# Narrower logit tiles, and softmax sums and weighted values issued behind the next window's logits

## The chip, the cores and the metric

The kernel runs on one core of a Trainium2 chip. The metric is the device time of one execution in microseconds. The engines go by their short names: PE is the matrix engine, PEld its weight loads, DVE the vector engine, ACT the scalar engine, POOL the general one, and SP the engine whose queue issues most of the DMAs.

## The reference

The input is `x`, four images of 128 channels and 64x64 pixels in float32. The first layer normalises over channels, adds a 3x3 depthwise convolution, and cuts each image into sixteen 16x16 windows. In every window, for two branches of four heads of 32 channels, each pixel attends to its 5x5 neighbours inside the window:

```python
q = einsum('ncij,bhdc->nbhdij', xw, Wq)          # k and v likewise
logits = einsum('nbhdij,nbhdkij->nbhkij', q, patches(k, 5)) * HD ** -0.5
attn = softmax(logits, axis=3)                   # over the 25 neighbours
o = einsum('nbhkij,nbhdkij->nbhdij', attn, patches(v, 5))
x = x + mix_of_branches(einsum('nbhdij,bhcd->nbcij', o, Wo))
```

Neighbours that fall outside the window have a key of zero, so they add one each to the softmax sum and nothing to its values.

The second layer takes the pixels of an image as 4096 tokens: linear attention with elu+1 features and a cumulative state, `t = t + attn(ln(t))`, and then a recurrent layer over all tokens, `t = t + rnn(ln(t))`, whose input is batch-normalised.

## The kernel before

An image is cut into four bands of 16 rows (`bands`, 16 in all) and a band into four windows (`places`, 64 in all; `wj` is the window's place in its band). One pass of the main loop, called an iteration here and named by the `wj` of the window `i` whose logits it computes, works on several windows at once: logits of window `i`, sums and weighted values of window `i-1` (`weighted`), the division by the sums for window `i-2` (`scaled`), and the projections q, k, v of window `i+1` (`window_inputs`).

- `logits` adds a mask product (L377, bfloat16) and six products of keys and queries for each head (L382, float32) in one PSUM bank per head. A head's 32 channels use 32 rows of PE, and the 128 keys of a block all its 128 columns. ACT takes the exponential of each bank (L391, `es`).
- `weighted` multiplies `es` by ones for the softmax sums (L400) and by the values (L412), both on all 128 rows with 32 columns a head. ACT copies the sums out (`den`, L403) and the values (`o_sb`, L420). A DMA folds `den` to 128x16 (`dc`, L405), DVE adds the count of outside neighbours and inverts (L423 to L427), a DMA writes the result to DRAM (`rd`, L429) and another spreads it back over 128 partitions (`rden`, L431). `weighted` is a generator of three parts: the sums, the values, and the way from `dc` to `rden`.
- `scaled` multiplies `o_sb` by `rden` on POOL (L440), one iteration later, into `oT`, a band's attention output.
- The layer-1 work of a finished band is a list of 24 steps in `layer1`: output product (`output0`, L465, which reads `oT` of all four windows, and the sum L472), norms (`measure`: L191, L193 on DVE, L195, L196 on POOL; `norm`: L203), transposes (L212), features (L494, L496, L498, L499), scores (L537, L539), values (L511, L519), states (L554, L562), `attend` (L573, L575, and on DVE L583, L584, L587), `keep` (L212, L592, a store) and `product` (L602, L603, L604). It begins in the iteration with `wj=1`.
- The norm and convolution of the next band (`front`) is another such list; its eight taps a half band on DVE are L288 (`y`), and ACT copies the finished half (`y2w`, L324).
- `between(i, gap)` takes the next step of both lists. There are six gaps in an iteration. L400 stands between gaps 0 and 1, L412 between gaps 1 and 2, and the three parts of `window_inputs` (q and k at L337, v at L350 with two DMAs of `v_sb` at L359 and L360) ahead of gaps 3, 4 and 5.

`in_order` pins the order in which PE, DVE, ACT and POOL instructions were written; SP's queue and the PSUM banks (one pool of eight, `bank`) are placed by the scheduler. `rden`, `den` and `oT` have one buffer each. After the main loop a recurrent part runs for about 100 us; it is not touched.

Of the kernel before, what the change touches and what calls it, by code (L numbers as in the profile page):

```python
# [17 lines left out]
P = 128  # L18
# [4 lines left out]
WT = WS * WS  # L23
BR, HEADS, HD = 2, 4, 32
KR = 2
BLOCKS = ((0, 6, 0), (6, 10, 4), (10, 16, 8))
BAND = WS * W
NCH = BAND // P
# [18 lines left out]
def conv_attn_hybrid(ctx: ExitStack, tc: tile.TileContext, ins: dict, out: bass.AP):  # L47
    nc = tc.nc
# [9 lines left out]
    def loaded(name, shape, dt=F32, src=None, eng=None):  # L58
        t = const.tile(shape, dt, name=name)
        (eng or nc.sync).dma_start(t, ins[name] if src is None else src)  # L60
        return t
# [34 lines left out]
    def load_head(n):  # L96
        b, wi = bands[n]
        heads[n] = p1.tile([P, P], F32, tag="head", name="head")
        nc.sync.dma_start(heads[n], ins["xt"][b, wi, :, 0, :])
# [18 lines left out]
    mask_k = loaded("mask_k", [P, P], BF16, eng=nc.scalar)  # L118
    mask_q = loaded("mask_q", [P, BR * WT], BF16, eng=nc.scalar)
# [56 lines left out]
    def bank():  # L176
        return ps.tile([P, 512], F32, tag="bank", name="bank")

    def run(g):
        for _ in g:  # L180
            pass
# [181 lines left out]

    pieces = [(br, n) for br in range(BR) for n in range(len(BLOCKS))]

    def spans(br, n):
        r0, r1, key0 = BLOCKS[n]
        return slice(br * WT + r0 * WS, br * WT + r1 * WS), br * WT + key0 * WS

    def logits(w):  # L370


        sps = [bank() for _ in range(HEADS)]
        for h in range(HEADS):
            rows = slice(h * HD, (h + 1) * HD)

            nc.tensor.matmul(sps[h], mask_k[rows], mask_q[rows], start=True, stop=False)  # L377
        for br, n in pieces:
            cols, k0 = spans(br, n)
            for h in range(HEADS):  # L380
                rows = slice(h * HD, (h + 1) * HD)
                nc.tensor.matmul(  # L382
                    sps[h][:, cols],
                    w["k"][rows, k0 : k0 + P],
                    w["q"][rows, cols],
                    start=False,
                    stop=(br, n) == pieces[-1],
                )
        for h in range(HEADS):
            es = p2.tile([P, BR * WT], F32, tag=f"es{h}", name=f"es{h}")  # L390
            nc.scalar.activation(es, sps[h], AF.Exp, scale=scale)  # L391
            w["es", h] = es

    def weighted(w):


        ops, dps = bank(), bank()
        for h in range(HEADS):
            rows = slice(h * HD, (h + 1) * HD)
            nc.tensor.matmul(dps[rows], ones[:, :HD], w["es", h], start=True, stop=True)  # L400

        den = p1.tile([P, BR * WT], F32, tag="den", name="den")
        nc.scalar.copy(den, dps)  # L403
        dc = p2.tile([P, 16], F32, tag="dc", name="dc")
        nc.sync.dma_start(dc, den[::HD, :])  # L405
        yield
        for br, n in pieces:
            cols, _ = spans(br, n)
            for h in range(HEADS):
                rows = slice(h * HD, (h + 1) * HD)  # L410
                c0 = br * P + h * HD
                nc.tensor.matmul(  # L412
                    ops[rows, cols],
                    w["v"][:, n, c0 : c0 + HD],
                    w["es", h][:, cols],
                    start=(br, n) == pieces[0],
                    stop=(br, n) == pieces[-1],
                )
        o_sb = p2.tile([P, BR * WT], F32, tag="o_sb", name="o_sb")
        nc.scalar.copy(o_sb, ops)  # L420
        yield

        nc.vector.tensor_tensor(dc, dc, pad_c, ALU.add)  # L423
        rc = p2.tile([P, 16], F32, tag="rc", name="rc")
        nc.vector.reciprocal(rc, dc)
        nc.vector.tensor_tensor(dmax, dmax, dc, ALU.max)
        nc.vector.tensor_tensor(dmin, dmin, dc, ALU.min)  # L427
        rd = dram4.tile([HEADS, BR * WT], F32, tag="rd", name="rd")
        nc.sync.dma_start(rd.rearrange("h (a e) -> (h a) e", e=16), rc)  # L429
        rden = p1.tile([P, BR * WT], F32, tag="rden", name="rden")  # L430
        nc.sync.dma_start(rden, rd.unsqueeze(1).to_broadcast([HEADS, HD, BR * WT]))  # L431
        w["o"], w["rden"] = o_sb, rden
        yield
# [174 lines left out]
    def layer1(n, last):  # L608

        a, c = Half(n, 0), Half(n, 1)  # L610
        y, z = last
        order = [
            (keep, z), None,
            (norm, z), (product, y), None,
            (output0, a), (measure, a), None,
            (turn_last, z), None,
            (norm, a), (output0, c), (measure, c), None,
            (turn, a), None,
            (product, z), (norm, c), None,
            (queries, a), None,  # L620
            (keys, a), None,
            (turn, c), None,
            (values, a), None,
            (queries, c), None,
            (scores, a), None,
            (keys, c), None,
            (turn_keys, a), None,
            (values, c), None,
            (accumulate, a), None,
            (turn_keys, c), None,  # L630
            (attend, a, 0), None,
            (attend, a, 1), (measure, a), None,
            (scores, c), (keep, a), None,
            (accumulate, c), (norm, a), None,
            (attend, c, 0), None,
            (turn_last, a), (attend, c, 1), (measure, c), None,
        ]
        for what in order:
            if what is None:
                yield  # L640
            elif what[1] is not None:
                what[0](*what[1:])
        halves[n] = a, c
# [15 lines left out]
    places = [(n, wj) for n in range(len(bands)) for wj in range(NB)]  # L659
# [27 lines left out]
    windows = {0: {}}  # L687
# [4 lines left out]
    def between(i, gap):  # L692


        next(behind, None)
        if i < len(places) and (i == 0 or i % NB or gap in (0, 2, 4)):
            next(ahead, None)

    for i in range(len(places) + 2):
        if i < len(places):  # L700
            n, wj = places[i]
            if i and wj == 0 and n + 1 < len(bands) and bands[n + 1][1] < NB - 1:
                load_head(n + 2)
            logits(windows[i])
        if 2 <= i:
            m, wjm = places[i - 2]
            if wjm == NB - 1:
                run(behind)
                behind = layer1(m, halves.pop(m - 1, (None, None)))
        between(i, 0)  # L710
        if 2 <= i:
            scaled(m, wjm, windows.pop(i - 2))
        if i < len(places) and wj == 1 and n + 2 < len(bands):
            load(n + 2)
        sums = weighted(windows[i - 1]) if 1 <= i <= len(places) else iter(())
        for gap in (1, 2):
            next(sums, None)
            between(i, gap)
        run(sums)
        if i == 0:  # L720
            run(fourth)
        inputs = iter(())
        if i + 1 < len(places):
            windows[i + 1] = {}
            inputs = window_inputs(windows[i + 1], *places[i + 1])
        for gap in (3, 4, 5):
            next(inputs, None)
            between(i, gap)
        run(inputs)
    run(behind)  # L730
    run(layer1_end(*halves.pop(len(bands) - 1)))
# [82 lines left out]
    for r, (s, counts) in enumerate(rounds):  # L814
# [4 lines left out]
        for g, (c0, c1) in enumerate(halves):  # L819
# [6 lines left out]
                start=False,  # L826
                stop=True,
# [621 lines left out]
def _neighbours():  # L1449
# [6 lines left out]
    for a in range(NQT):  # L1456
        for q in range(QT):
            r, c = a * QROWS + q // WS, q % WS
            n = 0
            for y in range(max(r - KR, 0), min(r + KR, WS - 1) + 1):  # L1460
                for x in range(max(c - KR, 0), min(c + KR, WS - 1) + 1):
                    band[:, q, a, (y - QKEY0[a]) * WS + x] = 0.0
                    n += 1
            pad_n[:, q, a] = (2 * KR + 1) ** 2 - n
    pad_n = pad_n.reshape(P, NQT)
# [3 lines left out]
def _masks():  # L1469
# [10 lines left out]
    pad = np.zeros((1, BR, WT), np.float32)  # L1480
    for r0, r1, key0 in BLOCKS:
        for q in range(r0 * WS, r1 * WS):
            r, c = divmod(q, WS)
            for i in range(8):
                queries[:, i, :, q] = 0.0 if abs(key0 + i - r) <= KR else -BIG
            for j in range(WS):
                queries[:, 8 + j, :, q] = 0.0 if abs(j - c) <= KR else -BIG
            rows = min(r + KR, WS - 1) - max(r - KR, 0) + 1
            cols = min(c + KR, WS - 1) - max(c - KR, 0) + 1
# [57 lines left out]
```

## Time and profile before

| | us |
|---|---|
| median of 3 runs | 929.56 (928.55 to 930.22) |
| profiled execution, first to last instruction | 933.3 |
| PE busy | 878.8 (94% of the span) |
| DVE busy | 734.2 (79%) |
| ACT busy | 539.5 (58%) |
| POOL busy | 257.5 (28%) |
| POOL idle until `rden` has landed, L440 | 221.5, in 29 waits |

No other time of the profiled execution is given, so its own time is taken to be the span, 933.3 us; that is 3.7 us above the median of the runs. The first row comes from runs, the others from one profiled execution. In lines of the profile "128x512 f32 x4" is the shape and the number of instructions; a mean or a duration follows, and brackets name idle time of the engine just ahead and who ended it. Float32 products are two instructions each on PE. A line of the table by stretches gives the stretch, its length, the busy time and number of instructions of PE, PEld, DVE, ACT and POOL, the granted PE clock as a share of full speed, and the DMA share with its GB/s.

### The profile page before, as it was taken

How to read it: one execution, taken by the hardware profiler on the slowest of the kernel's cores; microseconds unless marked ns; L12 is line 12 of the kernel's file. 1: busy time of each engine (PE TensorE's matmuls, PEld its weight loads, DVE VectorE, ACT ScalarE, POOL GpSimd, SP SyncE). 2: the span in 40 equal slices, each digit the busy share in tenths (PEclk: the TensorE clock that was granted, in tenths of full speed). 3: DMA queues.
4: the chain of work that ended last, by engine and by line, in shares of the span. 5: the costliest groups of instructions: out<-in, count | busy, mean ns of one | idle time of the engine just before them, and what ended most of it. 6: DMA issues, size and time to landing. Idle time of an engine off the chain costs nothing.

```text
span 933.3 us, 26460 instructions
## 1 busy us (share of the span) xinstructions
PE 878.8 (94%) x10508; PEld 657.1 (70%) x10508; DVE 734.2 (79%) x2408; ACT 539.5 (58%) x1010; POOL 257.5 (28%) x358
## 2 busy tenths in 40 slices
PE   4968999999999999999999999999999999977894
PEld 3846787777787777778777777777777778755452
DVE  6454888889797879798888889787878787577694
ACT  3654656575656565665657575656666565522553
POOL 2112141323222232314132323323231403131174
PEclk9988999999999999999999999999999999989898
DMA  4111112122212121211212121212121111111853
GB/s 121 25 46 57 42 51 58 56 59 63 59 48 61 48 66 49 73 38 57 55 54 60 59 60 48 62 51 65 48 71 37 60 36 56 36 35 32 351 223 143
DMA packets 53045, 63.46 MB, mean 68 GB/s; under 512 B 22960, under 2 KB 33840, under 8 KB 52400
## 3 DMA queue, kind: packets, MB, share of 16 engines
q1 hardware_dynamic: 51184, 56.91, 19.6%
q10 hardware_dynamic: 1728, 4.77, 1.3%
q8 instruction: 85, 1.39, 0.7%
q14 instruction: 48, 0.39, 0.1%
HBM read 35.44 MB, written 17.30 MB: 57 GB/s over the span
## 4 chain that ended last, share of the span: by engine, by line
PE 59%; DVE 25%; DMA 5%; ACT 3%; issue 3%; POOL 3%; ACTq 0%; SPq 0%; DVEq 0%; POOLq 0%
DVE y L288 9%; PE bank L337 9%; PE bank L465 7%; PE bank L382 6%; PE bank L212 6%; PE bank L494 5%; PE bank L400 4%; PE bank L350 4%; PE bank L412 3%; PE bank L602 3%; DMA res<-resd 2%; DVE st L191 2%; PE bank L537 2%; DVE state L562 2%; DVE x L587 2%
## 5 line engine op out<-in xcount | busy, mean ns | idle before, releaser
L288 DVE SCALAR_TENSOR_TENSOR y<-ypad,cpe_w,y 128x512 f32<-128x512 f32 x240 | 191.5, 798 | 17.4 <-ACT y L286 13.9
L391 ACT ACTIVATE es<-bank 128x512 f32<-128x512 f32 x256 | 132.2, 603 | 77.3 <-PE bank L382 77.3
L440 POOL TENSOR_TENSOR oT<-o_sb,rden 128x512 f32<-128x512 f32 x64 | 83.9, 1311 | 247.3 <-DMA rden<-rd 221.5
L195 POOL TENSOR_SCALAR rs<-mv 128x4 f32<-128x4 f32 (+2 forms) x100 | 25.0, 250 | 366.1 <-DVE mv L193 162.8
L203 DVE TENSOR_SCALAR xn<-x,mv,rs 128x128 f32<-128x128 f32 x256 | 89.5, 411 | 26.5 <-POOL rs L196 26.5
L196 POOL TENSOR_TENSOR rs<-rs,mhalf 128x4 f32<-128x4 f32 (+2 forms) x100 | 106.3, 1063 | 8.3
L382 PEld LDWEIGHTS bank<-q,k 32*128 32x128 f32 x3072 | 97.8, 189 | 9.7 <-ACT k L345 8.5
L382 PE MATMUL bank<-q,k 32*128 32x96 f32 (+1 forms) x3072 | 96.3, 271 | 1.1 <-ACT k L345 1.1
L412 PEld LDWEIGHTS bank<-es,v_sb 128*32 128x32 f32 x3072 | 56.5, 110 | 30.0 <-issue 19.6
L465 PE MATMUL bank<-woT,oT 128*128 128x128 f32 x512 | 67.1, 287 | 6.8 <-POOL oT L440 6.8
L465 PEld LDWEIGHTS bank<-woT,oT 128*128 128x128 f32 x512 | 63.8, 200 | 10.8 <-POOL oT L440 8.5
L494 PE MATMUL bank<-xl,awT 128*128 128x512 f32 x128 | 70.0, 630 | 0.0
L412 PE MATMUL bank<-es,v_sb 128*32 128x96 f32 (+1 forms) x3072 | 69.7, 239 | 0.0
L337 PE MATMUL bank<-y2w,wqT 128*128 128x256 f32 x256 | 68.2, 390 | 1.0 <-DVE y2w L288 1.0
L357 ACT COPY v_sb<-bank 128x512 f32<-128x512 f32 x64 | 37.5, 586 | 54.7 <-PE bank L350 48.0
L400 PE MATMUL bank<-es,ones 128*32 128x512 f32 x512 | 68.9, 611 | 0.0
L337 PE MATMUL bank<-y2w,wkT 128*128 128x256 f32 x256 | 66.9, 385 | 0.0
L350 PE MATMUL bank<-wvT,y2w 128*128 128x256 f32 x256 | 66.4, 382 | 0.0
L345 ACT COPY q<-bank 128x512 f32<-128x512 f32 x64 | 37.6, 587 | 43.3 <-PE bank L337 41.2
L345 ACT COPY k<-bank 128x512 f32<-128x512 f32 x64 | 37.3, 583 | 37.6 <-PE bank L337 37.6
L191 DVE BATCH_NORM_STATS2 st<-x 128x6 f32<-128x128 f32 x256 | 55.5, 280 | 1.1
L337 PEld LDWEIGHTS bank<-y2w,wqT 128*128 128x128 f32 x256 | 46.7, 198 | 13.0 <-issue 7.2
(118 smaller groups left out, 1719.7 us busy)
## 6 DMA issues: line engine op xcount, KB each, us to landing
rden<-rd SPq DMA_DIRECT2D x64, 256.0 KB
v_sb<-v_sb SPq DMA_DIRECT2D x128, 64.0 KB
resd<-rs_o SPq DMA_DIRECT2D x32, 256.0 KB
out<-ot SPq DMA_DIRECT2D x32, 256.0 KB
xin<-in_xt SPq DMA_DIRECT2D x15, 512.0 KB
res<-resd SPq DMA_DIRECT2D x2, 2048.0 KB
res<-resd ACTq DMA_DIRECT2D x2, 2048.0 KB
dc<-den SPq DMA_DIRECT2D x64, 8.0 KB
```

Source lines behind the costliest of these rows:

```text
L196: nc.gpsimd.tensor_tensor(rs[:, :n], rs[:, :n], mhalf[:, :n], ALU.pow)
L203: nc.vector.tensor_scalar(xn[:, j, :], piece, mv[:, j, 0:1], rs[:, j : j + 1], ALU.subtract, ALU.mult)
L288: nc.vector.scalar_tensor_tensor(y2, src, cpe_w[:, tap : tap + 1], y2, ALU.mult, ALU.add)
L337: nc.tensor.matmul(pps[:, br * WT : (br + 1) * WT], wT[:, br * P : (br + 1) * P], y2, start=True, stop=True,)
L350: nc.tensor.matmul(vps[:, e * 256 : (e + 1) * 256], y2[:, e * P : (e + 1) * P], wvT, start=True, stop=True,)
L382: nc.tensor.matmul(sps[h][:, cols], w["k"][rows, k0 : k0 + P], w["q"][rows, cols], start=False, stop=(br, n) == pieces[-1],)
L391: nc.scalar.activation(es, sps[h], AF.Exp, scale=scale)
L400: nc.tensor.matmul(dps[rows], ones[:, :HD], w["es", h], start=True, stop=True)
L412: nc.tensor.matmul(ops[rows, cols], w["v"][:, n, c0 : c0 + HD], w["es", h][:, cols], start=(br, n) == pieces[0], stop=(br, n) == pieces[-1],)
L440: nc.gpsimd.tensor_tensor(oTs[n][:, :, :, wj * WS : (wj + 1) * WS], w["o"].rearrange("p (a r c) -> p a r c", a=BR, c=WS), w["rden"].rearra ...
L465: nc.tensor.matmul(yps[:, j * P : (j + 1) * P], oT[:, br, t], woT[:, br, :], start=br == 0, stop=br == BR - 1,)
L494: nc.tensor.matmul(zps, awT[:, m * P : (m + 1) * P], h.xl, start=True, stop=True)
```

## The change

The masks and logits are issued as tiles of 32 rows by 64 columns, so that each of their products becomes two, one for each half of the keys, into the two halves of the bank's partitions. The first `yield` of `weighted` is taken out, so its first part now holds the sums and the values. That part is run directly behind `logits`, ahead of gap 0, and its last part (`dc` to `rden`) behind gap 3.

```diff
+KC = 64
...
         for h in range(HEADS):
             rows = slice(h * HD, (h + 1) * HD)
 
-            nc.tensor.matmul(sps[h], mask_k[rows], mask_q[rows], start=True, stop=False)
+            for c in range(0, P, KC):
+                nc.tensor.matmul(
+                    sps[h][c : c + KC],
+                    mask_k[rows, c : c + KC],
+                    mask_q[rows],
+                    start=True,
+                    stop=False,
+                )
         for br, n in pieces:
             cols, k0 = spans(br, n)
             for h in range(HEADS):
                 rows = slice(h * HD, (h + 1) * HD)
-                nc.tensor.matmul(
-                    sps[h][:, cols],
-                    w["k"][rows, k0 : k0 + P],
-                    w["q"][rows, cols],
-                    start=False,
-                    stop=(br, n) == pieces[-1],
-                )
+                for c in range(0, P, KC):
+                    nc.tensor.matmul(
+                        sps[h][c : c + KC, cols],
+                        w["k"][rows, k0 + c : k0 + c + KC],
+                        w["q"][rows, cols],
+                        start=False,
+                        stop=(br, n) == pieces[-1],
+                    )
...
         nc.sync.dma_start(dc, den[::HD, :])
-        yield
         for br, n in pieces:
...
             logits(windows[i])
+        sums = weighted(windows[i - 1]) if 1 <= i <= len(places) else iter(())
+        next(sums, None)
         if 2 <= i:
...
-        sums = weighted(windows[i - 1]) if 1 <= i <= len(places) else iter(())
         for gap in (1, 2):
-            next(sums, None)
             between(i, gap)
-        run(sums)
...
         for gap in (3, 4, 5):
             next(inputs, None)
             between(i, gap)
+            run(sums)
         run(inputs)
```

## The prediction

> **What bounds the kernel now.** I read the page's busy times first, then a table of one band cut at its four L377 starts, then the order of time of PE, DVE, POOL and SP in that band, and last the waits.
>
> ```profile
> PE 878.8 (94%) x10508; PEld 657.1 (70%) x10508; DVE 734.2 (79%) x2408; ACT 539.5 (58%) x1010; POOL 257.5 (28%) x358
> ...
> 312.46:326.42 13.96, 13.55 (x175) 11.06 (x174) 13.26 (x58) 7.36 (x14) 4.70 (x7) 1.00 0.18 55
> ...
> sum 50.07, PE 49.66 PEld 37.95 DVE 42.55 ACT 30.84 POOL 13.57; mean PE 12.42 PEld 9.49 DVE 10.64 ACT 7.71 POOL 3.39
> ```
>
> A band lasts 50.07 us and PE is busy in 49.66, so PE bounds it. But DVE needs 42.55, and in the iteration with wj=0 (the line 312.46) it is busy 13.26 of 13.96 us: there two engines are full at once. DVE's order of time shows where it waits in a band; two of these waits open its long runs:
>
> ```profile
> 293.96 0.69 DVE L604 BATCH_NORM_STATS2 stats<-wx 128x6 f32<-128x512 f32 x1 [1.79 <-ACT wx L603]
> ...
> 303.98 0.74 DVE L288 SCALAR_TENSOR_TENSOR y<-ypad,cpe_w,y 128x512 f32<-128x512 f32 x1
> ...
> 306.86 0.43 DVE L498 TENSOR_SCALAR low<-low 128x512 f32<-128x512 f32 x1 [1.54 <-ACT low L496]
> ...
> 319.44 0.61 DVE L587 SCALAR_TENSOR_TENSOR x<-bank,rd,x 128x128 f32<-128x128 f32 x2
> ```
>
> From L498 at 306.86 to the end of L587 at 320.05 it has no gap: 13.19 us of queue. PE's order of time shows who waits for that, SP's and POOL's the way from dc to the output product:
>
> ```profile
> 312.69 1.48 PE L382 MATMUL bank<-q,k 32*128 32x96 f32 x48
> 314.10 0.71 PE L573 MATMUL bank<-v,aT 128*128 128x129 f32 x4
> 314.96 1.07 PE L400 MATMUL bank<-es,ones 128*32 128x512 f32 x8
> 317.05 1.09 PE L412 MATMUL bank<-es,v_sb 128*32 128x96 f32 x48
> 318.07 1.16 PE L537 MATMUL bank<-f,f 128*128 128x128 f32 x8
> 319.85 0.59 PE L212 MATMUL bank<-ident,x 128*128 128x128 f32 x2 [0.41 <-DVE x L587]
> ```
> ```profile
> 322.40 0.14 DVE L423 TENSOR_TENSOR dc<-dc,pad_c 128x16 f32<-128x16 f32 x1
> 322.86 0.33 SPq L429 DMA_DIRECT2D rd<-rc  x1
> 324.35 0.57 SPq L431 DMA_DIRECT2D rden<-rd  x1
> 325.46 0.51 SPq L359 DMA_DIRECT2D v_sb<-v_sb  x1
> 330.46 1.28 POOL L440 TENSOR_TENSOR oT<-o_sb,rden 128x512 f32<-128x512 f32 x1
> 332.48 2.05 PE L465 MATMUL bank<-woT,oT 128*128 128x128 f32 x16
> ```
> ```profile
> POOL oT L440 <- DMA rden<-rd: 221.5, 29, 13.6
> ```
>
> The reader is to see that oT ends at 331.74 and PE takes it at 332.48: 0.74 us of slack on PE's clean run, behind a DMA on which POOL waits 221.5 us in all.
>
> [...] L400 streams two rounds of 512 columns side by side, and one round takes 0.43 us (a pair of L494 starts 0.43 apart), 0.86 in all; it takes 1.00 to the next start. I read 0.10 us a switch. [...] L382's 12 rounds of four products need 1.41 us, 0.117 each, though L412's 12 rounds over the same columns with 32-column weights need only 1.02. [...] late in the trace L465 starts after 2.46 us of idle and its 16 products take 3.78 us, against 2.05 at 332.48.
>
> **The change, part by part.**
>
> PE's work. L382 becomes 96 products on 64-column tiles. If the eight tiles of a round run together, [...] the run takes what L412 does, about 1.04 instead of 1.41: -0.37. The switches: into and out of the tiled modes six times now, three times after: -0.28. Sum -0.65 us a window, 41.6 us over 64 windows. This is the saving if PE were the only bound. L377 stays (its four products run side by side, 0.23 from its start to L382's).
>
> The order. L400 and L412 leave the gaps between layer-1 steps and stand ahead of all of them: the first step's product starts 3.16 us after L377 (0.23+1.04+0.90+0.99 for the runs start to start) instead of 1.64. ACT's den and o_sb copies stand ahead of these steps' copies. On DVE the dc sums (L423 to L427, 0.54 us) move behind one y (wj=2), behind L519 and two y (wj=3), and in wj=0 behind L562 x4 and L203 xn x4; in wj=1 they stay. On SP rd moves behind the v_sb copies or between them; dc's own DMA leaves earlier and has landed long before it is read. In wj=2 and wj=3 rden comes 1.5 to 3 us later too and oT waits for it on POOL; behind it stands an rs that is not due until 8 us later (POOL idles 12.33 us before the oT at 307.79, and its next rs starts at 319.25), so I price that at nothing; without that cover it would hold up the xf transposes. PSUM banks: the built order frees every bank that L377, L400 and L412 take before I expect it to be used; I price that at nothing, cover 0.6 us at the tightest (the value sums L519 ahead of L537).
>
> So I follow the band's loop through the engine that is late, each link from the lines above and their like, before -> after:
>
> a) L465 to the L377 of wj=2: 332.48 to 339.72, PE busy throughout, untouched: 7.24 -> 7.24.
> b) That L377 to stats L604: 4.31 now. After: es starts at 1.34 (0.23+0.91+0.2 until the logits are seen), then ACT starts: four es at 0.486 each, den 0.52, o_sb 0.5, wx 0.62 long, stats 0.03 on: 4.97. +0.66: the earlier logits are eaten by den and o_sb ahead of wx.
> c) L604 to the end of the eighth y: 293.96 to 304.72, DVE full: 10.76 -> 10.76. Moving dc within it changes nothing.
> d) To L498: 2.14 now; after, ACT's y2w follows y by 0.19, low follows 0.51 later and takes 0.69: 1.42. -0.72.
> e) L498 to the end of L587, call it X: 13.19 -> 13.19.
> f) X to L465: 12.43 now, bound by PE. After, by PE: q at X+0.22, to the next L377 5.9, then 3.16, keep, xf and product y 2.3: X+11.6. By rden: the DVE items from X to L562 now take 2.81 with dc's 0.46 in them; L562 starts at X+2.35, xn ends at X+4.7, dc and rc at X+5.1. SP first issues L359, which waits for the v_sb copy (PE's v at X+3.74, copy done 1.64 later), so rd goes at X+5.93 instead of X+2.81. rden follows 1.45 later, as now (1.49), lands 5.2 later (issued 302.56, oT freed by it at 307.79), oT takes 1.28, PE 0.05: X+13.9. +1.5, and PE idles 2.3 us at L465.
>
> Sum of a loop: 7.24+4.97+10.76+1.42+13.19+13.9 = 51.5 against 50.1: +1.45. The trace holds 14 such loops (L377 of wj=2 at 88.85 to 790.87): +20 us. PE's 2.6 us a band become idle time: here, and before keep's transposes, where PE is back 0.65 earlier than now and L587 later.
>
> Clock: not shown in the steady part of the trace. At most one window of 3.4 us a loop at half speed in link (a), 1.7 us x 14 = 24; at least 0, if 2.3 us of idle is too short; a gain has no cause. I take 8, [...].
>
> Edges: before 88.85 PE's six windows save up to 0.65 each, and DVE's y no longer queue behind dc: between 0 and -4, I take -2. After 790.87 the last L465 already waited 2.46 for oT and dc now stands behind xn: +2. Sum 20+8 = 28. The profiled span is 933.3, 3.7 above the median 929.56; the change is added to the median: **958 us**.
>
> **The rivals.**
> *Not slower: rden lands in time.* One link, f: if rd or rden came back faster, or POOL took oT sooner, by 2.3 us, PE's own X+11.6 would hold. The loop is then 49.2, -0.9 x 14 = -13, with the start 915. It turns at rden landing 3.8 us after its issue. For it: oT of wj=1 comes 6.1 us after the issue now, bound by POOL's rs, so its landing is not seen. Against: all landings on which POOL does wait are 5 us or more. 13%.
> *PE alone decides:* 929.6-41.6 = 888. Against: DVE's 13.19 us without a gap, ahead of which PE already waits. 2%.
> *Tiles don't run together:* the change doesn't do what it says; halves load one after the other or 96 pairs issue at L412's 21 ns: 2.04 instead of 1.04. es is 1.0 later in b: 14 more, 972. For it: nothing here issues faster than L412. Against: in the single starts of L412 a round of 64 columns takes 0.056 for four loads and four products, the time of its columns alone, and queued instructions start 3.3 ns apart. 15%.
> *Clock halves in every band, in both gaps:* 24 and as much again before keep: 985 and above. 10%.
>
> **How the numbers follow.** The main case (rden late, tiles together) has 60%, its own range 945 to 975: 20 with +-5 for landing (5.0 to 5.6) and 0 to 24 for the clock. The slower rivals reach to 985; faster cases lie at 915 and 888. Range 936 to 984. Within 0.2% (1.9 us, about what a measurement here can tell) only if f is misjudged by 1.4: 3%. Faster 15%, slower 82%.
>
> **What would show it.** Right: a band of 51.5 to 53 us; L465 idle 2 us and more behind oT in each band; rd behind L359 in wj=0; stats 5 us after L377; L382's run near 1.04 us; PE busy below 93% in the middle slices. Wrong: L465 starting without a wait, or bands of 49 us (step f); L382 near 2 us (the tiles); PEclk at 10 throughout with bands over 53 (the clock).

## The result, and the profile after

| | before | after |
|---|---|---|
| median of runs, us | 929.05 (927.71 to 930.22, 4 runs) | 977.8 (973.04 to 980.23, 4 runs) |
| ratio to before, 95% interval | | 1.052 (1.0493 to 1.0546) |
| profiled execution, span, us | 933.3 | 971.3 |

The changed kernel is 5.2% slower, 49 us by the medians and 38 us by the two profiled executions. The profiled one was the quickest of its four, so some 11 us of the difference by the medians can't be looked up in a trace. Most lines of the code moved by 8 (L465 is now L473, L377 is L379, L382 is L391, L400 is L409, L412 is L420, L429 and L431 are L437 and L439, L440 is L448, L604 is L612), those ahead of `logits` by 1.

From the page of the changed kernel, busy times and the granted PE clock in 40 slices:

```profile
PE 861.0 (89%) x13836; PEld 666.2 (69%) x13836; DVE 721.8 (74%) x2408; ACT 538.7 (55%) x1010; POOL 259.1 (27%) x358
...
PEclk9987999999999999999999999899999999979798
```

PE is busy for 18 us less, with 3328 instructions more, and the kernel is longer: PE waits. The table by stretches, one stretch for each band from one L379 of wj=2 to the next (stretch, length, busy time and number of instructions of PE, PEld, DVE, ACT and POOL, PE clock, DMA share, GB/s):

```profile
296.91:347.97 51.06, 47.50 (x850) 37.93 (x850) 41.28 (x142) 30.72 (x57) 13.73 (x19) 1.00 0.19 55
...
559.10:613.38 54.28, 49.68 (x854) 39.80 (x853) 42.91 (x150) 31.63 (x59) 15.23 (x22) 0.97 0.19 54
613.38:672.50 59.12, 51.16 (x853) 40.25 (x853) 41.44 (x144) 31.24 (x58) 13.76 (x19) 0.94 0.17 48
...
sum 740.02, PE 683.03 PEld 543.09 DVE 583.31 ACT 433.81 POOL 194.95; mean PE 48.79 PEld 38.79 DVE 41.67 ACT 30.99 POOL 13.93
```

Fourteen bands take 740.02 us; they took 702.02. The difference, 38.0, is that of the spans: what lies ahead of the first of them is 2.08 shorter (86.77 against 88.85), what lies behind the last 2.08 longer (144.51 against 142.43). Eight bands ran at full clock throughout and take 51.4 on average, six hold one or two stretches of 3.4 us at half clock (the 0.97 and 0.94) and take 54.8. Against the 50.14 of before, 1.3 in each of the fourteen bands makes 18 of the 38 us, and the longer six add 20.

The place where the time goes is shown by the order of time of one band. DVE, SP, POOL and PE in wj=0 and wj=1:

```profile
377.88 0.61 DVE L595 SCALAR_TENSOR_TENSOR x<-bank,rd,x 128x128 f32<-128x128 f32 x2
...
383.29 0.59 ACT L358 COPY v_sb<-bank 128x512 f32<-128x512 f32 x1 [1.17 <-PE bank L351]
383.75 0.16 DVE L431 TENSOR_TENSOR dc<-dc,pad_c 128x16 f32<-128x16 f32 x1
383.90 0.51 SPq L360 DMA_DIRECT2D v_sb<-v_sb  x1
...
384.50 0.53 SPq L437 DMA_DIRECT2D rd<-rc  x1
...
385.07 0.50 SPq L361 DMA_DIRECT2D v_sb<-v_sb  x1
...
386.20 0.57 SPq L439 DMA_DIRECT2D rden<-rd  x1
...
391.15 1.27 POOL L448 TENSOR_TENSOR oT<-o_sb,rden 128x512 f32<-128x512 f32 x1 [0.35 <-DMA rden<-rd]
...
392.48 0.71 PE L473 MATMUL bank<-woT,oT 128*128 128x128 f32 x4 [1.60 <-POOL oT L448]
```

X, the end of L595, is 378.49. `dc` is inverted only at 384.2 and `rd` goes at X+6.0, between the two `v_sb` DMAs; `rden` follows 1.7 later, POOL takes it 4.95 after its issue, and PE starts L473 0.05 after `oT`, having idled 1.60. In the band that the prediction shows, the same product started 0.74 after `oT` and without a wait. The list of waits says the same of the whole run:

```profile
POOL oT L448 <- DMA rden<-rd: 232.3, 47, 16.0
...
PE bank L473 <- POOL oT L448: 39.0, 16, 6.1
```

The first output product of each of the sixteen bands now waits for `oT`; before, PE waited for it five times, 6.8 us in all. POOL's wait grew by only 11 us; what changed is that PE has no other work that covers it.

The other new wait is ahead of `stats` in wj=2, PE, ACT and DVE in order of time:

```profile
347.97 0.42 PE L379 MATMUL bank<-mask_q,mask_k 32*64 32x512 bf16 x8
...
348.21 1.39 PE L391 MATMUL bank<-q,k 32*64 32x96 f32 x96
349.50 2.07 ACT L400 ACTIVATE es<-bank 128x512 f32<-128x512 f32 x4 [0.79 <-PE bank L391]
349.52 1.07 PE L409 MATMUL bank<-es,ones 128*32 128x512 f32 x8
350.41 1.07 PE L420 MATMUL bank<-es,v_sb 128*32 128x96 f32 x48
351.40 1.12 PE L610 MATMUL bank<-xl,fwT 128*128 128x512 f32 x2
351.43 0.62 ACT L412 COPY den<-bank 128x512 f32<-128x512 f32 x1
351.89 0.64 ACT L428 COPY o_sb<-bank 128x512 f32<-128x512 f32 x1
...
352.57 0.59 ACT L611 COPY wx<-bank 128x512 f32<-128x512 f32 x1
353.19 0.69 DVE L612 BATCH_NORM_STATS2 stats<-wx 128x6 f32<-128x512 f32 x1 [2.70 <-ACT wx L611]
```

DVE idles 2.70 us until `wx`, which stands behind four exponentials, `den` and `o_sb`. The logits run takes 1.31 from its start to the next run's (348.21 to 349.52).

The loop cut into the links of the prediction, in us, over 13 bands (the first of the fourteen has no `stats` of its own). The lines named are those of the changed kernel:

| link | before, mean | forecast | after, median | after, mean |
|---|---|---|---|---|
| a) L473 to L379 of wj=2 | 7.26 | 7.24 | 7.24 | 7.75 |
| b) to `stats` L612 | 4.31 | 4.97 | 5.22 | 5.55 |
| c) to the end of the eighth `y` | 10.69 | 10.76 | 10.24 | 10.45 |
| d) to L506 | 2.20 | 1.42 | 1.74 | 1.78 |
| e) to X | 13.05 | 13.19 | 13.20 | 13.03 |
| f) X to L473 | 12.72 | 13.9 | 14.28 | 14.41 |
| sum | 50.2 | 51.5 | 51.9 | 53.0 |

### The profile page after: what moved, and what is told of

Its sections match the earlier page's. It is cut to its first block, busy times and chain, and to the rows that moved or that the text cites. A ratio compares the mean times of both kernels' runs of the same rounds, so it can differ in the third digit from the quotient of the medians.

```text
span 971.3 us, 33056 instructions
## 1 busy us (share of the span) xinstructions
PE 861.0 (89%) x13836; PEld 666.2 (69%) x13836; DVE 721.8 (74%) x2408; ACT 538.7 (55%) x1010; POOL 259.1 (27%) x358
## 4 chain that ended last, share of the span: by engine, by line
PE 48%; DVE 24%; DMA 13%; ACT 5%; POOL 4%; issue 4%; SPq 1%; ACTq 0%; POOLq 0%; DVEq 0%
DVE y L289 8%; PE bank L338 8%; DMA rden<-rd 8%; PE bank L473 7%; PE bank L502 5%; PE bank L391 4%; PE bank L351 4%; PE bank L409 3%; PE bank L213 3%; PE bank L420 3%; DVE st L192 3%; POOL oT L448 2%; DMA res<-resd 2%; DVE state L570 2%; DVE x L595 2%
## 5 line engine op out<-in xcount | busy, mean ns | idle before, releaser
L448 POOL TENSOR_TENSOR oT<-o_sb,rden 128x512 f32<-128x512 f32 x64 | 83.8, 1309 | 319.2 <-DMA rden<-rd 232.3
L400 ACT ACTIVATE es<-bank 128x512 f32<-128x512 f32 x256 | 132.2, 603 | 63.8 <-PE bank L391 63.8
L473 PE MATMUL bank<-woT,oT 128*128 128x128 f32 x512 | 72.8, 302 | 39.0 <-POOL oT L448 39.0
L473 PEld LDWEIGHTS bank<-woT,oT 128*128 128x128 f32 x512 | 69.2, 214 | 45.1 <-POOL oT L448 44.4
L204 DVE TENSOR_SCALAR xn<-x,mv,rs 128x128 f32<-128x128 f32 x256 | 74.7, 354 | 29.8 <-POOL rs L197 29.7
L420 PEld LDWEIGHTS bank<-es,v_sb 128*32 128x32 f32 x3072 | 64.1, 111 | 45.1 <-issue 40.9
L391 PE MATMUL bank<-q,k 32*64 32x96 f32 (+1 forms) x6144 | 89.9, 247 | 5.8 <-ACT k L346 5.8
L391 PEld LDWEIGHTS bank<-q,k 32*64 32x64 f32 x6144 | 88.1, 132 | 9.2 <-ACT k L346 6.7
L420 PE MATMUL bank<-es,v_sb 128*32 128x96 f32 (+1 forms) x3072 | 71.1, 238 | 4.8 <-issue 4.7
L409 PE MATMUL bank<-es,ones 128*32 128x512 f32 x512 | 69.1, 612 | 0.0
L480 DVE TENSOR_TENSOR x<-bank,xin 128x512 f32<-128x512 f32 x32 | 21.9, 686 | 61.8 <-PE bank L473 61.8
L612 DVE BATCH_NORM_STATS2 stats<-wx 128x6 f32<-128x512 f32 x32 | 22.2, 694 | 56.1 <-ACT wx L611 56.0
L502 PE MATMUL bank<-xl,awT 128*128 128x512 f32 x128 | 63.5, 598 | 0.0
```

The source lines that it names most:

```text
L204: nc.vector.tensor_scalar(xn[:, j, :], piece, mv[:, j, 0:1], rs[:, j : j + 1], ALU.subtract, ALU.mult)
L391: nc.tensor.matmul(sps[h][c : c + KC, cols], w["k"][rows, k0 + c : k0 + c + KC], w["q"][rows, cols], start=False, stop=(br, n) == pieces[-1],)
L420: nc.tensor.matmul(ops[rows, cols], w["v"][:, n, c0 : c0 + HD], w["es", h][:, cols], start=(br, n) == pieces[0], stop=(br, n) == pieces[-1],)
L448: nc.gpsimd.tensor_tensor(oTs[n][:, :, :, wj * WS : (wj + 1) * WS], w["o"].rearrange("p (a r c) -> p a r c", a=BR, c=WS), w["rden"].rearra ...
L473: nc.tensor.matmul(yps[:, j * P : (j + 1) * P], oT[:, br, t], woT[:, br, :], start=br == 0, stop=br == BR - 1,)
L502: nc.tensor.matmul(zps, awT[:, m * P : (m + 1) * P], h.xl, start=True, stop=True)
```

## The experiments

The theory (A in the quoted expectations) is the prediction's: `rden` comes late in link f, by DVE's order and SP's, and half clock follows PE's idle time there now and then (seven stretches of 3.41 us at a granted clock of 0.50 in the 14 loops of the changed kernel). Rivals: the 96 small products cost more than 48 (B), PE alone decides (C), or the place of sums and values ahead of the first layer-1 step is what costs (D). X is the end of L595, as above. Ratios are to the kernel before on the same chip; medians of different rows come from different chips, so steps between rows are best read from the ratios.

| kernel | median, us | ratio (95%) |
|---|---|---|
| e1_tiles_only | 925.4 | 0.9963 (0.9950 to 0.9977) |
| e2_order_only | 980.9 | 1.057 (1.052 to 1.062) |
| e3_tail_gap2 | 951.3 | 1.023 (1.018 to 1.028) |
| e4_fill | 999.0 | 1.074 (1.070 to 1.079) |
| e5_tail_vact | 946.9 | 1.021 (1.017 to 1.025) |
| e6_fill_half | 977.3 | 1.054 (1.050 to 1.058) |
| e7_vact | 961.5 | 1.037 (1.031 to 1.044) |
| e8_sums_gap1 | 936.7 | 1.011 (1.007 to 1.015) |
| e9_e5_fill | 947.1 | 1.019 (1.016 to 1.022) |
| e10_e8_fill | 941.9 | 1.014 (1.010 to 1.018) |
| e11_tiles_lessdve | 911.3 | 0.981 (0.978 to 0.983) |
| e12_fill_first | 944.2 | 1.016 (1.013 to 1.018) |

**Tiles alone, order alone.** e1_tiles_only has the tiles and the order of before; e2_order_only is the changed kernel with

```diff
-KC = 64
+KC = 128
```

> Only the tiles: the masks and logits in 32x64 tiles, all else in the order of the kernel before. Theory A (the changed kernel is late because rden comes late in link f and because PE's idle time halves the clock; the tiles are no cause): the logits run takes about 1.22 us to its last product as in the changed kernel, 0.19 less than before; one such run lies in link b and one in link f of the kernel before, so the band gets 0.4 shorter, 14 x 0.4 = 5: 924 us, range 917 to 929. Theory B (96 small products a window cost more than 48): slower than before, 940 and above. Theory C (PE alone decides): 64 x 0.19 = 12 less, 917.

> Only the order: sums and values directly behind the next logits and the last part of weighted behind gap 3, but logits in 128-column tiles as before. Theory A: as slow as the changed kernel or slower, since the path through rden is the same and es comes up to 0.2 us later in link b: 975 to 990 us, oT late at the output product by 1.5 us and more in each band, five to nine windows of half clock. Theory B (the tiles cost): near 930.

Both came out as theory A has them: 925.4 for 924, 980.9 in 975 to 990. The tiles are worth -0.4%, the order carries the whole loss, and B falls; so does C, whose 917 lies below e1's interval (924.4 to 926.9, by its ratios). In e1 links b and f are shorter, b 4.11 (4.31 before), f 12.64 (12.72).

**The last part of `weighted` back behind gap 2.** e3_tail_gap2:

```diff
         for gap in (1, 2):
             between(i, gap)
+        run(sums)
...
             between(i, gap)
-            run(sums)
         run(inputs)
```

> The changed kernel with one thing undone: the last part of weighted (dc, rc, rd, rden) stands behind gap 2 again, ahead of gap 3 and of the v_sb DMAs; sums and values stay as one run ahead of gap 0. Theory A: link f falls from 14.3 to what PE needs, 11.6 to 12.0, PE no longer idles 1.5 us and more at the output product, and windows of half clock go with it; loop 5.2+10.3+1.7+13.2+11.9+7.2 = 49.5 against 50.14, 14 x -0.6 = -9: 920 us, range 912 to 928. Theory D (the run of sums and values ahead of the first layer-1 step is the cause, through ACT's and DVE's later start): still 945 or more. Theory B: still 960 or more.

951.3: half of the loss is gone, and it is 31 us over the forecast. `rd` went at X+2.8 to X+3.07 in all bands but the last, where it had been before the change, but SP's queue in order of time shows a `v_sb` DMA between it and `rden`:

```profile
377.43 0.33 SPq L437 DMA_DIRECT2D rd<-rc  x1
381.44 0.51 SPq L360 DMA_DIRECT2D v_sb<-v_sb  x1
382.06 0.55 SPq L439 DMA_DIRECT2D rden<-rd  x1
```

The scheduler places SP's issues, and it put L360 ahead of L439; L360 waits for ACT's copy, 3.7 us, and `rden` behind it. In nine of the 14 bands `rden` follows `rd` only after 3.0 us (three) or 4.6 us (six); link f is 14.0 to 14.7 in these six, and 12.77 in the median of 13 bands, for 14.28 in the changed kernel and 11.6 to 12.0 in the forecast. The edit undid DVE's half of the delay, and SP's not in these nine. Link e grew as well, from 13.03 to 13.76 on average.

**SP's half.** e5_tail_vact adds the following to e3, e7_vact adds it to the changed kernel:

```diff
-        nc.sync.dma_start(v_sb[:64, 1, :], v_sb[64:, 0, :])
-        nc.sync.dma_start(v_sb[64:, 1, :], v_sb[:64, 2, :])
+        nc.scalar.dma_start(v_sb[:64, 1, :], v_sb[64:, 0, :])
+        nc.scalar.dma_start(v_sb[64:, 1, :], v_sb[:64, 2, :])
```

> As e3_tail_gap2 (the last part of weighted behind gap 2), and the two v_sb DMAs of a window issued by ACT, which makes the v_sb copy, instead of SP. In e3 rd went at X+3.06 as before, but rden 4.6 us later in most bands, because SP's queue has a v_sb DMA between them that waits for the copy. Theory A2 (link f is late by SP's queue as well as by DVE's order): rden follows rd by 1.5, link f 11.6 to 12.0 in all bands, loop 5.2+10.1+1.9+13.2+11.9+7.2 = 49.5, some windows of half clock left behind keep's gap of 1.36 us: 915 to 932, 922 likeliest. Rival (rden's landing or PE's own order keeps f above 13, or ACT's issuing of DMAs costs as much): 940 and above.

> The changed kernel with the v_sb DMAs issued by ACT and nothing else; the last part of weighted stays behind gap 3. It parts SP's share of link f from DVE's. By link: rc is done at X+5.1 and rd no longer waits for the v_sb copy, rd at X+5.2 instead of X+6.0, rden 1.5 behind it instead of 1.7 to 3.3, landing 5.2, oT 1.28: f 13.2 instead of 14.28. 14 x -1.1 = -15, and two or three windows of half clock fewer, -5 to -8: 945 to 965, 957 likeliest. Rival (SP's queue is the whole cause of f): f 12, 930. Rival (DVE's order is the whole cause): 970 to 982.

e7 came out at 961.5 for 957, inside its range: `rd` goes at X+5.3 to 5.9 in all but the last band, `rden` 1.44 to 1.51 behind it in nine of 13 bands, and f is 13.73 in the median. e5 did to `rden` what was claimed:

```profile
376.51 0.33 SPq L437 DMA_DIRECT2D rd<-rc  x1
...
377.95 0.53 SPq L439 DMA_DIRECT2D rden<-rd  x1
...
380.52 0.47 ACTq L360 DMA_DIRECT2D v_sb<-v_sb  x1
```

`rden` follows 1.44 behind here and 1.44 to 1.52 in all 13 bands. Link f is 11.5 to 12.3 in six of the eight bands that ran at full clock throughout, and 13.2 to 14.2 in the five with a window of half clock in that link. Its best band takes 49.48, the forecast loop. Yet it takes 946.9, not 922: its bands average 51.3, with b at 5.88 (4.31 before) and e at 13.37. Theory A as it stood is too small; the next runs ask what else there is. Nor do the two halves add up: SP's is worth 1.5% with DVE's in place (the changed kernel against e7), but once DVE's is undone, e5 is only 0.2% ahead of e3, and the intervals overlap.

**Sums and values behind the first layer-1 step.** e8_sums_gap1 is e5 with

```diff
-        sums = weighted(windows[i - 1]) if 1 <= i <= len(places) else iter(())
-        next(sums, None)
         if 2 <= i:
...
             scaled(m, wjm, windows.pop(i - 2))
...
+        sums = weighted(windows[i - 1]) if 1 <= i <= len(places) else iter(())
+        next(sums, None)
         for gap in (1, 2):
```

> As e5_tail_vact, but sums and values, still one run, stand behind the layer-1 step of gap 0 instead of ahead of it. ACT's wx is then ahead of den and o_sb: link b falls from 5.22 to 4.1 (4.31 before less the shorter logits run), the rest as e5; one more switch a window, 0.1 each, lies on PE's links. Theory A2: loop 48.4 to 49.0, 908 to 920, 914 likeliest, faster than e5 by 5 to 14. Theory D (what costs is not the place ahead of the layer-1 step): e5's time within 0.3%.

936.7, 10 less than e5: b is 4.52 in the median, 5.53 in e5, so D has its share. The size of the step was right, the level was not: 936.7 for 914. The runs spread from 929.8 to 942.9, and the profiled one, the quickest, has links of 50.1 in sum, for 50.2 in the kernel before.

**The clock.** e4_fill adds products, whose results nothing reads, to the changed kernel where PE idles, ahead of L473 and between the pairs of transposes of `keep`; e6_fill_half has about half of them. This is e6's edit:

```diff
         yps = bank()
+        if h.s == 0:
+            for _ in range(2):
+                nc.tensor.matmul(yps[:, : 3 * P], ident, awT, start=True, stop=True)
...
         for j in range(n):
+            if j == 2:
+                for _ in range(fill):
+                    nc.tensor.matmul(tps[:, 2 * P :], ident, awT[:, : 2 * P], start=True, stop=True)
...
-        nc.scalar.copy(rs, turned(h.x, 0, 4).rearrange("p (k s) -> p s k", s=SEG))
+        nc.scalar.copy(rs, turned(h.x, 0, 4, 2).rearrange("p (k s) -> p s k", s=SEG))
```

> The changed kernel with idle time of PE filled: four added products of 384 columns (1.28 us) ahead of each band's first output product, into the bank that this product overwrites, and five of 256 columns (1.07 us) between the two pairs of transposes of keep. Nothing else moves, and the results are unchanged. Theory A (half of the loss is clock: seven windows of half clock in the steady part, six of them behind these two gaps, each costing its band 2 to 3.3 us and one 7.7): the windows of half clock go, 15 to 20 us less than the changed kernel: 957 to 963, rden as late as there. Rival (the clock is not set by PE's idle share, or its loss would have been waited for anyway): 973 to 982, as the changed kernel. Rival (the fill itself is in the way): above 982.

> The changed kernel with half of the fill of e4, since a float32 product of 384 columns takes 0.65 us and not 0.32: two of 384 columns (1.3 us) ahead of each band's first output product, two of 256 columns (0.86 us) between the two pairs of transposes of keep. The idle times there are 1.5 us and more, and 1.36. Theory A (clock): the added products fit into the idle time, no window of half clock is left in the steady part, bands of 51.1 to 51.9 as in the undisturbed bands of the changed kernel: 955 to 963, 958 likeliest. Rival (the loss of the disturbed bands would have been waited for anyway): 973 to 982.

e4 was slower, 999, by its own fill, which I had sized at half its length: ahead of L479 it takes 2.58 us, from its start to L479's, where I had 1.28. PE of e4 in order of time, wj=1; L475 is the fill, and `oT` is ready at 350.51, before it starts:

```profile
347.37 2.32 PE L215 MATMUL bank<-awT,ident 128*128 128x256 f32 x10
...
351.37 2.75 PE L475 MATMUL bank<-awT,ident 128*128 128x384 f32 x8
353.95 1.28 PE L479 MATMUL bank<-woT,oT 128*128 128x128 f32 x10
```

e6 is the better test. From 100 to 800 us only one window of half clock is left, and link a is 7.25 on average instead of 7.75. The time is 977.3, that of the changed kernel: f grew from 14.41 to 14.68 on average and d from 1.78 to 1.91, and `rden` left 2.3 after `rd` on average instead of 2.1. In 11 of its 14 bands the output product (L479 there) still starts 0.05 or 0.06 after `oT`, so there the fill was not in its way. That the half-clocked windows lengthen link a is shown; that the kernel loses time by them is not.

e9_e5_fill and e10_e8_fill put the two products of `keep` into e5 and e8, e12_fill_first into e5 and a band's first half alone. The edit of e12 against e9:

```diff
-        nc.scalar.copy(rs, turned(h.x, 0, 4, 2).rearrange("p (k s) -> p s k", s=SEG))
+        nc.scalar.copy(rs, turned(h.x, 0, 4, 0 if h.s else 2).rearrange("p (k s) -> p s k", s=SEG))
```

> e5_tail_vact with two added products of 256 columns (0.86 us) between the two pairs of transposes of keep, where PE idles 1.36 us in each band; results unchanged. In e5 link f is no longer bound by rden, and five of its seven windows of half clock lie behind that idle time, so the clock is tried by itself here. Theory A (clock): these windows go; each cost its band about 1.7 us, some more where it delayed the next copies: e5's 946.9 falls by 8 to 12, 936 to 940. Rival (the loss would have been waited for anyway, as e6 suggests): 943 and above.

> The same two products added to e8_sums_gap1. Its runs spread from 929.8 to 942.9, the fastest with a granted clock of 0.985 and the others with 0.976 to 0.980. Theory A: the spread is windows of half clock; with them gone the runs gather near the fastest, 928 to 933, 930 likeliest, and the order is then still no faster than the kernel before, since the undisturbed bands of e8 (50.1 mean) are those of before. Rival (the spread has another cause): median 935 and above.

> As e9_e5_fill, but the two added products stand only in the keep of a band's first half, where PE idles 1.36 us, and no longer in that of the second half, where it does not idle. In e9 link f was 13.15 us against 12.28 in e5's undisturbed bands, 0.87 us longer, as long as the two products: those of the second half stood on PE's own path. Theory A (clock): e9's 947.1 less 14 x 0.87 = 12: 935, range 931 to 939, so that the windows of half clock cost e5 about 12. Rival (the windows cost nothing, what follows a half-clocked band waits anyway): 943 to 949.

e9 (947.1) and e10 (941.9) are no faster than e5 (946.9) and e8 (936.7). PE of e9 in order of time, the first half's `keep` at 323 and the second half's at 386:

```profile
323.09 1.03 PE L215 MATMUL bank<-awT,ident 128*128 128x256 f32 x4
...
324.61 0.58 PE L216 MATMUL bank<-ident,x 128*128 128x128 f32 x2 [0.49 <-DVE x L598]
...
386.51 1.03 PE L215 MATMUL bank<-awT,ident 128*128 128x256 f32 x4
387.38 0.38 PE L216 MATMUL bank<-ident,x 128*128 128x128 f32 x2
```

The first fill lies in idle time, the second on PE's path, and f is 13.14 or 13.15 in nine of 13 bands. e10 has the same fault: its f is 13.34 in the median, 12.48 in e8, and 0.86 in each of 14 loops makes 12 us. So neither e9 nor e10 decides, and what spreads e8's runs stays open. e12 takes the second fill away, f is 12.28 in the median, as in e5's undisturbed bands, and the time is 944.2, in the rival's range and not in mine (931 to 939). Against e5 that is 2.6 us by the medians and 0.5% by the ratios, whose intervals just overlap, where I had put 12 for the windows of half clock. The traces say more for the clock: e12's has no window of half clock between 85 and 825 us, and its 14 loops take 708.3, e5's 717.4, so 9.1 less. But behind the last `stats`, in the recurrent part that the edit doesn't touch, the profiled execution of e12 takes 71.4 for e5's 68.1, and that hides a third of it. What the windows cost e5 is thus 2.6 by the medians and 9.1 by the loops of one execution each; the runs don't settle it.

**What else e5 and e12 lose.** PE stops inside a run for what the profile calls issue. The changed kernel, PE in order of time:

```profile
615.82 0.96 PE L420 MATMUL bank<-es,v_sb 128*32 128x96 f32 x41
619.15 0.55 PE L420 MATMUL bank<-es,v_sb 128*32 128x96 f32 x7 [2.37 <-issue]
```

Counted over 85 to 840 us, stops above 0.15 us in the weighted values (L420) sum to 4.7 us in the changed kernel (five), 5.5 in e3, 7.0 in e5, 5.4 in e7 and 4.1 in e12. There is one of 1.2 in e8 and one of 1.0 in e11 (below), and none in the kernel before, in e1 or in e2. The stop at 619.15 makes its band's b 8.98, and a half-clocked window follows it, in the band of 59.12. With e12's links b at 5.71 (4.31 before) and e at 13.40 (13.05), such stops and ACT's longer queue are what I can name of its 14 us.

**DVE as the next bound.** e11_tiles_lessdve is e1 with

```diff
-        nc.vector.tensor_tensor(dc, dc, pad_c, ALU.add)
...
-        nc.vector.tensor_tensor(dmax, dmax, dc, ALU.max)
-        nc.vector.tensor_tensor(dmin, dmin, dc, ALU.min)
```

> e1_tiles_only with three of the four DVE operations of the softmax sums left out: the count of outside neighbours is not added and the running maximum and minimum (a guard) are not kept, so 0.37 us less of DVE a window. e1 freed 0.19 us a window on PE, 12 us in all, and gained 4. Theory E (links c and e are DVE's queue, so what PE saves there is waited for): one such group lies in c and one in e; the band gets 0.74 shorter until PE binds again, 14 x 0.5 to 0.74 = -7 to -10: 915 to 919. Rival (PE still bounds the band, at 49.5 busy of 49.8): 922 to 926.

911.3, 14 us below e1 and below even the range. From the pages of e1 and of e11:

```profile
PE 869.7 (94%) x13836; PEld 646.0 (70%) x13836; DVE 734.5 (79%) x2408; ACT 539.3 (58%) x1010; POOL 257.8 (28%) x358
...
PE 860.4 (95%) x13835; PEld 645.5 (71%) x13836; DVE 708.4 (78%) x2216; ACT 538.9 (59%) x1010; POOL 257.8 (28%) x358
```

DVE had 26 us less to do. On average links e and f shorten by 0.6 and 0.3; c shortens by 0.5, but d grows by as much, so theory E holds for e and not for c. It also answers where the gain of the tiles went: links c to e, 26 of 50 us, take 26.0 in e1 and 25.9 in the kernel before, so what the tiles save PE there does not shorten the band.

## Why the prediction was right, and where it was off

The forecast was 958 in a range of 936 to 984, the result 977.8: slower, by the mechanism named, and nearer to the upper end than to the middle. What held, and what was off, link by link:

- **Switches and tiles.** Three switches instead of six: right; L420 follows L409, on tiles of the same shape, without a gap: 0.88 from start to start in all 56 cases between 85 and 820 us, where L400 took 1.00 before to a next run on 128x128 tiles, in all 59. L409 starts 0.17 after the last logits product, whose columns take 0.08, so 0.09 is left for the switch. That weight loads set the pace of L382, and that the logits run would take 1.04 on narrower tiles, was my estimate; the run takes 1.31. A weight load took 189 ns on average with 128 columns (L382), 132 with 64 (L391) and 111 with 32 (L420). The eight products of a round do start within 24 ns of each other, but only the first two rounds come every 0.08 us; from the third on, single products start some 17 ns apart. What sets that pace no run shows. So neither the likeliest case (the run takes what L412 takes) nor the rival (2.04) held.
- **Step b** (4.31 to 4.97): right in its chain, short by 0.25 in the median. `es` starts at 1.53 instead of 1.34, by the longer logits run; the rest of the mean's 5.55 is the one stop at 619.15. e8 confirms the place: behind the first layer-1 step, b falls by 1.0.
- **Step c**, "changes nothing", was 0.5 too long in the median: the `dc` sums that left it were on its path. **Step d** came out at 1.74 instead of 1.42, since `low` also waits for PE's L502, now behind L420 and L545, 0.36 us in the band that starts at 296.91; c and d together are 11.98 for a forecast of 12.18: two errors that nearly cancel. **Step e** and **step a** stand, 13.20 and 7.24 in the median.
- **Step f** (12.43 to 13.9) is the mechanism, and e3, e5 and e7 show both halves of it: with SP's alone undone (e7) the kernel gets 16 us quicker, with DVE's alone (e3) 27, with both (e5) 31. Its terms: `rd` at X+5.93 (measured 6.01 in the median), landing 5.2 (4.94 to 5.32). The term that was too small is the 1.45 from `rd` to `rden`: 1.67 to 3.30, 2.1 on average, 0.6 x 14 = 9 us. Where `rd` is issued 2.3 us or more ahead of the `v_sb` DMAs (before, e1, e5), the distance is 1.44 to 1.54 in all bands but the last; closer to them or between them, in the changed kernel, it is 1.67 and more. But in e7, with the `v_sb` DMAs 0.1 us behind `rd` on ACT's queue, it is 1.44 to 1.48 in most bands and 2.2 or 3.2 in others, so what makes it longer is not shown. PE idles 1.2 to 3.9 us at L473, 2.1 on average, for a forecast of 2.3.
- **Clock** (8 us, 0 to 24): the number of windows a loop and the 8 were my estimate. The trace before has half clock (0.50) only ahead of its steady part and behind it, in stretches of 3.41 us (at 81.60) to 10.24 (at 64.53); the one at 825.70, of 6.83, lies over the L465 that took 3.78. After: seven windows of 3.41 in 14 loops, not one a loop and not none. Four of them cost link a 1.6 each; another, in a link f, made ACT's copy of `v_sb` and with it `rd` 1.7 later. The six bands that hold the windows are 3.4 longer than the others, 20 us in all. But not all of that is the clock's: in five of the six `rden` leaves 2.2 to 3.3 behind `rd`, in seven of the eight others 1.7, and the wait for `oT` comes just ahead of four of the seven windows. With these windows gone but for one in e6, such a late `rden` remains and the time does not fall. So of this term only the occurrence is confirmed; the 8 us are not.
- **Edges** (-2, +2): -2.08 and +2.08.
- **The sum**: 14 loops cost 38.0 in the profiled execution for a forecast of 20+8. The eight bands at full clock take 51.4 for a forecast of 51.5, in part by luck: in them b and d are 0.3 and 0.4 longer than forecast on average, c, e and f 0.4, 0.3 and 0.2 shorter. The rest to the median's 49 lies in executions without a trace, and e8's runs spread by 13 us for a reason that I haven't found. Both stay open.

The rivals: `rden` did not land in time, and even e5, with link f near that rival's 11.6 in its undisturbed bands, did not come out faster than before: the rival's 915 left out b, PE's stops and the clock. PE alone did not decide: it is busy for 18 us less in a kernel that is 38 us longer. Undone in the order e7, e5, e8, e1, the loss of 5.2% goes in these steps of the ratios, in per cent: SP's place of `rd` 1.5, DVE's place of the last part 1.7, sums and values ahead of the first layer-1 step 1.0, the rest of that order (one run instead of two, and ACT's DMAs) 1.5, less 0.4 for the tiles. The split between the first two hangs on the order: with e3 ahead of e5, DVE's place is 2.9 and SP's 0.2.

Of the versions tried that compute everything, e1_tiles_only beats both kernels: 925.4, 0.4% below before.

## What to carry to other kernels

Time that an engine saves pays only in the stages where it ends last (in e1 PE is busy for 9 us less, and the kernel gains 4); cut the loop into links, name the late engine of each, and price a change there. When a step is moved, follow the small results that it sends out (here 16 columns of reciprocals) through every queue to their reader, the queue that a scheduler orders included, and ask for the slack at that reader: here it was 0.74 us, and the move made their DMA 3 us later. An experiment that fills idle time must put its fill only where the trace shows idle time, and take the length of the fill from the trace.

## What the runs showed of the hardware

**Half clock in the changed kernel.** All seven stretches of half clock of the changed kernel between 85 and 835 us last 3.41 us, at a granted clock of 0.50. They begin at 236.70, 431.26, 499.52, 605.34, 618.99, 663.36 and 755.52; from one to the next it is 57, 20, 31, 4, 13 and 27 times 3.4133 us, to 0.01 us. The table by stretches of the changed kernel, cut in such steps, windows in pairs, the second at half clock in the first and third pair:

```profile
233.29:236.70 3.41, 0.90 (x8) 0.90 (x9) 0.69 (x1) 1.19 (x3) 1.26 (x1) 1.00 0.28 95
236.70:240.11 3.41, 3.41 (x15) 3.12 (x14) 1.25 (x4) 0.00 (x0) 0.00 (x0) 0.50 0.00 0
182.09:185.50 3.41, 1.83 (x16) 1.83 (x17) 1.61 (x2) 0.32 (x1) 1.26 (x1) 1.00 0.10 30
185.50:188.91 3.41, 3.41 (x25) 3.15 (x25) 2.26 (x13) 1.83 (x4) 1.10 (x2) 1.00 0.03 6
...
427.85:431.26 3.41, 1.71 (x8) 1.30 (x9) 3.34 (x23) 0.78 (x2) 1.24 (x3) 1.00 0.20 69
431.26:434.67 3.41, 3.41 (x14) 3.06 (x13) 3.24 (x17) 0.59 (x1) 3.07 (x5) 0.50 0.21 77
```

Busy 0.90 and 1.71 us of 3.41 were followed by half clock, 1.83 was not. Over all windows so cut in the changed kernel's steady part (starts from 83 to 829 us), the seven busy shares that were followed by it are 0.02 to 0.50; of those that were not, one is 0.45 and all others 0.51 and more, so no exact threshold comes out. Nor does the length of an idle time of PE tell by itself: half clock came at the end of 2.37 us inside L420 (616.78 to 619.15), but not with 2.36 and 2.32 us ahead of L473 (to 446.11 and 183.67); of the thirteen idle times of 1.36 us between the transposes of `keep` it followed two, those that begin at 428.68 and 753.44.

**Stops of PE inside a run of small products.** The page counts 111 packets of 16 KB on one instruction queue (q8) where the kernel before has 85. Each of the changed kernel's five stops in L420 ends 2.2 to 2.6 us after such a packet started. e1, with as many PE instructions (13836), and e2, with the same order on the wide tiles (10508 instructions, 85 packets), don't stop above 0.15 us. Five to nine stops are seen where the 96 small products and the 56 of sums and values follow each other in one run (the changed kernel, e3, e5, e7, e12), one or two (e8, e10, e11) or none (e1) where a layer-1 step stands between them. That the stop is the wait for that packet is what the times suggest; no run took the packets away.
